# A first norm split by block, a planner that keeps GpSimd and VectorE apart, and tiles placed in the buffer that comes free first

## The chip, the core and the metric

The kernel runs on one core of one Trainium2 chip. Its time is the device time of one execution in microseconds; the times below are the median of several executions. The engines are TensorE (PE in the views; its weight loads are PEld), VectorE (DVE), ScalarE (ACT), GpSimd (POOL) and SyncE (SP, which only issues transfers here). ScalarE's queue issues some transfers as well.

## What is computed

One transformer block with the norm after each half, in float32: grouped-query attention with normed queries and keys and a distance bias, then a gated feed-forward with integer weights. Batch 2, sequence 512, width 512; 32 query heads, 8 key and value heads of 128; feed-forward width 1376.

```python
q = rmsnorm((x @ Wq.T) per head, q_norm_w);  k = rmsnorm((x @ Wk.T) per head, k_norm_w);  v = x @ Wv.T
scores = q k^T / sqrt(128) + (-1e30 above the diagonal, slope_h * (key - query) below it)
x = layernorm(x + (softmax(scores) v) @ Wo.T)
h = silu((x @ gate_w.T) * gate_s) * ((x @ up_w.T) * up_s)
out = layernorm(x + (h @ down_w.T) * down_s)
```

## The kernel before

**Units and pairs.** A unit is (group g, batch b, block i): the four query heads of one key and value head, and one block of 128 rows. Two units in a row make a pair, so there are 64 units and 32 pairs. A pair is projected together: 256 rows by 768 columns (four query heads, one K, one V).

**Seven products.** Nearly every projection is done as a two by two block product with seven multiplications in place of eight (`seven`, with `PLAN`). A product is named in the text by the first number of its row in `PLAN`; they are issued as 1, 2, 6, 7, 4, 5, 3. Products 1, 6, 7 and 4 add up in one PSUM bank (`pa`), 5 and 3 in another (`pb`), 2 has its own (`pc`); between them the bank is copied or added to SBUF, so product 6 waits for the copy of product 1. The factors need sums of blocks first: `sx` of the input, `tq` of the projection weights, `to` of the output weights, `so` of the attention output, `sw`, `tx`, `sh` and `td` in the feed-forward part. Those are two-input sums in SBUF, that VectorE or GpSimd can do (`sums_a`, `sums_b`, through `tensor`, L520).

**The first pair** is projected the plain way (`project_plain`, tiles `pp`): four banks, four chunks `kc` of the depth, for each chunk the blocks of rows r = 0, 1 and the halves of columns n = 0, 1. A float32 product of 384 columns is two matmul instructions.

**Norm of a pair** (`heads`): ScalarE squares the five heads of each block (L766), VectorE adds them up (`ms<-sq`, L775) and scales (L782), GpSimd raises to the power -1/2 (`inv<-ms`, L506), two multiplies give the normed heads (`sq<-c,inv`), and TensorE turns them (`ptq` for queries, L836; `ptk` for keys, L858). `qT` and `kT` are their copies.

**Attention of a unit**: four score products (`sc<-kT,qT`, L889), on each a bias add with row maximum on VectorE (L898), an exponential on ScalarE (L914), a rescale on GpSimd (`pr<-pr,rden`, L946), transposes (`pt`, L978), copies (`prT`), products with v (`pa<-prT,v`, L997). Then the output projection adds into `y`, and after the last group the layer norm follows.

**Feed-forward part.** For each of 11 chunks of the width and each batch: weights loaded as integers and cast (`wf`), sums `sw`, seven products (`pa_h`, `pb_h`, `pc_h`) whose banks are copied by ScalarE and added by VectorE into `gu`, a sigmoid (L1366), and two three-operand products of VectorE (`sg`, L1374; `hT`, L1383). A bank must be emptied before its next product.

**The order of work** is made by a planner, `Work`. The kernel records every operation with the engines that could do it, an estimated duration for each, and a priority. `emit` then steps through a list schedule: among all operations whose inputs are done it takes the one, and the engine, that can start earliest by the estimates, with priority as the next criterion, and issues it there. So each engine's instruction order is fixed when the program is built. The engines then run in their own order and wait for each other through semaphores; the estimates do not bind them. An operation that needs a new tile takes the next one of its ring (`Ring`), in turn; it has to wait until all users of the tile that held that place are done.

The planner's estimates for two-input sums in SBUF are `dve(n, sbuf=True)` on VectorE and `pool_tt(n)` on GpSimd; nothing in it knows of the two engines hindering each other.

**Loads at the start.** `load_qkv(0)` issues, for each chunk, the query weights of both halves as one transfer of 256 KB on SP, and on ACT's queue the input (`load_x`, 128 KB), the K and the V weights (64 KB each). A transfer takes one of eight semaphores in turn, so a ninth waits for the first to land. Meanwhile TensorE does 16 idle transposes (`idle`, tile `warm`).

Of the kernel before, what the change touches and what calls it, by code (L numbers as in the profile page):

```python
# [58 lines left out]
def dve(n, sbuf=False):  # L59
    return 0.2 + 0.0014 * n if sbuf else 0.15 + 0.00106 * n  # L60


def pool_tt(n):
    return 0.28 + 0.0021 * n


def pool_ts(n):
    return 0.3 + 0.00095 * n
# [6 lines left out]
class Ring:  # L75


    def __init__(self, name, bufs, shape, dtype=F32, gate=None):
        self.name, self.bufs, self.shape, self.dtype = name, bufs, shape, dtype
        self.gate = gate  # L80
        self.pool = None
        self.items = []
# [14 lines left out]
class Work:  # L97
# [6 lines left out]
    def add(self, costs, prio, fn, reads=(), writes=(), after=(), table=None, lag=0.0):  # L104

        op = {
            "costs": costs,
            "prio": prio,
            "fn": fn,
            "deps": set(id(o) for o in after),  # L110
            "obj": list(after),
            "takes": [],
            "end": None,
            "table": table,
            "lag": lag,
            "n": len(self.ops),
        }
        deps = {id(o): o for o in after}
        for key in reads:
            o = self.wrote.get(key)  # L120
            assert o is not None, (key[0].name, key[1])
            deps[id(o)] = o
        for key in writes:
            o = self.wrote.get(key)
            if o is not None:
                deps[id(o)] = o
            for o in self.read.get(key, ()):
                deps[id(o)] = o
        for key in reads:
            if key not in writes:  # L130
                self.read.setdefault(key, []).append(op)
        for key in writes:
            self.wrote[key] = op
            self.read[key] = []
        bufs = []
        for key in list(reads) + list(writes):
            b = key[0]
            if b not in bufs:
                bufs.append(b)
        for b in bufs:  # L140
            op["takes"].append(b)
            b.users.append(op)
        op["deps"] = list(deps.values())
        self.ops.append(op)
        return op

    def emit(self):
# [20 lines left out]
        emitted = 0  # L168
        while ready:
            best = None  # L170
            for o in ready:
                t0 = o["at"]
                for b in o["takes"]:
                    if b.tile is not None:
                        continue
                    r = b.ring
                    if r.gate is not None and r.gate["end"] is None:
                        t0 = None
                        break
                    k = len(r.items) - r.bufs  # L180
                    if k >= 0:
                        for u in r.items[k].users:
                            if u["end"] is None:
                                t0 = None
                                break
                            t0 = max(t0, u["end"] + LAG[u["eng"]])
                        if t0 is None:
                            break
                if t0 is None:
                    continue  # L190
                for e, c in o["costs"].items():
                    s = max(t0, free.get(e, 0.0))
                    key = (s, o["prio"], s + c, o["n"])
                    if best is None or key < best[0]:
                        best = (key, o, e, c, s)
            assert best is not None, "no work can start: " + ", ".join(
                b.name for o in ready for b in o["takes"]
            )
            _, o, e, c, s = best
# [9 lines left out]
            elif e == "NONE":  # L209
                o["end"] = s  # L210
            else:
                free[e] = s + c
                o["end"] = s + c
            o["lag"] += LAG[e]
            for b in o["takes"]:
                if b.tile is not None:
                    continue
                b.ring.items.append(b)
                b.tile = b.ring.pool.tile(
                    b.ring.shape, b.ring.dtype, tag=b.ring.name, name=b.name, bufs=b.ring.bufs  # L220
                )
# [11 lines left out]
def post_ln_block(  # L233
# [122 lines left out]
    def load_qkv(g, prio):  # L356
# [3 lines left out]
        for kc in range(NK):  # L360
            load(
                0.26,
                prio + 0.01 * kc,
                lambda q, kc=kc: q.dma_start(w[:, kc, :, : 2 * HD], src[:, kc]),
                [(w, ("q", kc))],
            )
            if g == 0:
                load_x(0, kc, 0, prio + 0.01 * kc, "ACTQ")
                for n, other in enumerate((wkt, wvt)):
                    load(  # L370
                        0.066,
                        prio + 0.01 * kc + 0.001,
                        lambda q, kc=kc, n=n, other=other: q.dma_start(
                            w[:, kc, n, 2 * HD :], other[ts(kc, P), ts(g, HD)]
                        ),
                        [(w, ("kv", n, kc))],
                        queue="ACTQ",
                    )
# [12 lines left out]
    def load_x(b, kc, q, prio, queue="SP"):  # L391

        c0 = q * NTH
        load(
            0.13,
            prio,
            lambda e: e.dma_start(
                xT[b][:, kc, c0 : c0 + NTH], xt[ts(kc, P), b * S + c0 : b * S + c0 + NTH]
            ),
            [(xT[b], (kc, q))],  # L400
            queue=queue,
        )

    def w_keys(g, kcs, ns=(0, 1)):
        w = w_qkv[g]
        return [(w, ("q", kc)) for kc in kcs] + [(w, ("kv", n, kc)) for kc in kcs for n in ns]
# [20 lines left out]
    def idle(e):  # L427
        for k in range(16):
# [3 lines left out]
    W.add({"PE": 3.3}, -9.0, idle, [A(ident)], [A(warm)])  # L432
# [54 lines left out]

    def make_bias(g, prio):
        bg = Buf(r_bias, f"bias_{g}")
        bias[g] = bg  # L490
        for h in range(G):
# [7 lines left out]
                [(bg, h)],  # L499
            )  # L500

    def rsqrt(dst, src, n, prio, dst_key, src_key):
# [6 lines left out]
            [src_key, A(nhalf)],  # L509
            [dst_key],  # L510
# [4 lines left out]
    def tensor(n, prio, dst, a, b, alu, reads, writes, who=("DVE", "POOL"), sbuf=None, after=()):  # L515
        cost = {"DVE": dve(n, len(who) > 1 if sbuf is None else sbuf), "POOL": pool_tt(n)}
# [6 lines left out]
            after,  # L523
        )

    def sums_a(n, prio, s, a, s_key, a_keys):
# [5 lines left out]
        tensor(n, prio, g(0), f(1, 0), f(1, 1), add, k(1, 0) + k(1, 1), [s_key(0)])  # L532
        tensor(n, prio, g(2), f(0, 0), f(1, 0), sub, k(0, 0) + k(1, 0), [s_key(2)])
        tensor(n, prio, g(1), g(0), f(0, 0), sub, [s_key(0)] + k(0, 0), [s_key(1)])
        tensor(n, prio, g(3), f(0, 1), g(1), sub, k(0, 1) + [s_key(1)], [s_key(3)])
# [57 lines left out]
    def sums_x(b, q, prio):  # L593
        def blocks(r, k):
# [10 lines left out]
            lambda r, k: [(xT[b], (2 * k, q)), (xT[b], (2 * k + 1, q))],  # L605
# [17 lines left out]
    def sums_o(g, prio):  # L623
# [9 lines left out]
            lambda r, n: [A(w)],  # L633
        )
# [5 lines left out]
    def copy_op(n, prio, dst, src, reads, writes, who=("ACT", "DVE")):  # L640
# [6 lines left out]
        cost = {"ACT": act(n), "DVE": dve(n), "POOL": 0.2 + 0.00095 * n}  # L647
        W.add({e: cost[e] for e in who}, prio, fn, reads, writes)

    def project_plain(p, prio):  # L650
# [7 lines left out]
        for kc in range(NK):  # L658
            for (r, n), bank in banks.items():
# [10 lines left out]
                reads = [(xT[b], (kc, i // 2))] + w_keys(g, (kc,), (n,)) + ([A(bank)] if kc else [])  # L670
                W.add({"PE": pe(W3)}, prio + 0.01 * kc, mm, reads, [A(bank)])
# [10 lines left out]
    def project(p, prio):  # L682
# [50 lines left out]
        def a_keys(f):  # L733
            if isinstance(f, tuple):
                return [(xT[b], (2 * f[1], i // 2)), (xT[b], (2 * f[1] + 1, i // 2))]
# [14 lines left out]
    def heads(p, prio):  # L750
# [10 lines left out]
        nh = 2 * (G + 1)  # L761
        for r in range(2):
# [9 lines left out]
        W.add(  # L772
            {"DVE": 1.5},
            prio,
            lambda e: nc.vector.tensor_reduce(ms.tile, sq.tile, AX.X, ALU.add),  # L775
            [(sq, 0), (sq, 1)],
            [A(ms)],
        )
        W.add(
            {"DVE": 0.2},  # L780
            prio,
            lambda e: nc.vector.tensor_scalar(  # L782
                ms.tile, ms.tile, 1.0 / HD, RMS_EPS, ALU.mult, ALU.add
            ),
            [A(ms)],
            [A(ms)],
        )
        rsqrt(
            lambda: inv.tile.rearrange("p r h -> p (r h)"),
            lambda: ms.tile.rearrange("p r h -> p (r h)"),  # L790
            nh,
            prio,
            A(inv),
            A(ms),
        )
        for r in range(2):
# [7 lines left out]
                [(cb, (r, 0)), (cb, (r, 1)), A(inv)],  # L804
# [153 lines left out]
    def attend(u, prio):  # L958
# [68 lines left out]
        def halves(e):  # L1027
# [11 lines left out]
            {"PE": 0.7},  # L1039
# [87 lines left out]
    def layernorm(t, prio, dst, dst_keys, name):  # L1127
        stats, mv = Buf(r_stats, f"stats_{name}"), Buf(r_mv, f"mv_{name}")
        ve, rstd = Buf(r_ve, f"ve_{name}"), Buf(r_rstd, f"rstd_{name}")
        for n in range(2):  # L1130
# [21 lines left out]
        rsqrt(lambda: rstd.tile, lambda: ve.tile, 1, prio, A(rstd), A(ve))  # L1152
# [7 lines left out]
            dst_keys,  # L1160
        )
# [42 lines left out]
    for p in range(NP):  # L1204
# [7 lines left out]
        if p == 0 or g != pairs[p - 1][0]:  # L1212
            sums_q(g, u - 3.0)
            sums_o(g, u + 1.0)
        if p == 0:
            project_plain(p, u - 2.4)
        else:
            if g == 0 or (g == 1 and b == 0 and i == 0):
                sums_x(b, i // 2, u - 3.0)
            project(p, u - 2.4)  # L1220
        heads(p, u - 1.8)
        for k in range(2):
# [84 lines left out]
    def ffn_up(fc, b, weights, prio):  # L1307
# [52 lines left out]
        def finish():  # L1360
# [17 lines left out]
                [A(sg)],  # L1378
            )
# [12 lines left out]
                [(h, (fc, 0)), (h, (fc, 1))],  # L1392
            )
# [197 lines left out]
```

## Time and profile before

| | |
|---|---|
| median of 3 runs | 1078.73 us (1078.64 to 1078.96) |
| the profiled execution | 1081.15 us, of which its span is 1079.4 us |
| TensorE's mean granted clock in it | 0.995 |
| busy: PE / DVE / POOL / ACT | 1059.0 / 687.2 / 514.8 / 408.3 us |
| transfers | 38.93 MB, mean 36 GB/s |
| first useful product (`pp`) | at 5.35 us |
| first score product (`sc`) | at 33.72 us |

The busy time of an engine is the union of its instructions. A matmul's record lasts longer than the time until the next one may start: a 128x384 product reads 0.49 us, and such products follow each other every 0.32 us. In a timeline line the first figure is the start from the beginning of the span, the second the length, and a bracket at the end gives the idle time of that engine before it and what ended it. In a line of windows the columns are the stretch, its length, the busy time of PE, PEld, DVE, ACT and POOL (with the number of instructions), the granted clock of TensorE as a share of full speed, the share of the transfer engines and GB/s.

### The profile page before, as it was taken

Reading aid. Unit: us, or ns where it says so; the run is one execution under the profiler, and the core shown is the slowest. Engines: PE = TensorE matmul, PEld = TensorE weight load, DVE = VectorE, ACT = ScalarE, POOL = GpSimd, SP = SyncE. Lnnn points to the kernel's source line nnn. Section 1 sums busy time; section 2 is a strip of 40 time slices with the busy share of each in tenths; the row PEclk is TensorE's granted clock in tenths of the full one; section 3 lists DMA queues with packets and bytes.
Section 4 is the critical chain, followed back from the end, with each engine's and each line's share of the span. In section 5 each row is a group of like instructions: output and inputs, shape, how many; then the busy total and the mean of one; then the engine's idle time right before and its main releaser. Section 6 shows DMA issues by size and latency. Waiting matters only on the chain.

```text
span 1079.4 us, 13367 instructions
## 1 busy us (share of the span) xinstructions
PE 1059.0 (98%) x4612; PEld 763.0 (71%) x4612; DVE 687.2 (64%) x1611; ACT 408.3 (38%) x1024; POOL 514.8 (48%) x673
## 2 busy tenths in 40 slices
PE   8999999999999999999999999999999999999997
PEld 5667676667666767676666766766667787877886
DVE  7665576656665666565656567657676667677554
ACT  2534444443344434443344334343444423433100
POOL 9364454445544453545355526554666443245130
PEclk9999999999999999999999999999999999999999
DMA  8210011001200120012001200100101012320011
GB/s 273 89 46 14 1 40 51 9 1 39 60 0 1 40 59 1 1 40 60 1 1 40 59 1 1 40 1 1 39 1 39 20 51 67 103 57 20 1 40 39
DMA packets 44146, 38.93 MB, mean 36 GB/s; under 512 B 3664, under 2 KB 36432, under 8 KB 44080
## 3 DMA queue, kind: packets, MB, share of 16 engines
q1 hardware_dynamic: 42352, 37.05, 11.2%
q10 hardware_dynamic: 1728, 1.05, 0.4%
q8 instruction: 36, 0.59, 0.2%
q14 instruction: 30, 0.25, 0.1%
HBM read 35.99 MB, written 2.10 MB: 35 GB/s over the span
## 4 chain that ended last, share of the span: by engine, by line
PE 92%; DVE 4%; DMA 2%; POOL 1%; issue 1%; ACT 0%; SPq 0%; POOLq 0%; DVEq 0%; ACTq 0%
PE pa_q L568 14%; PE sc L889 12%; PE pa_o L568 10%; PE pa L997 10%; PE pb_q L568 7%; PE pt L978 6%; PE pa_h L568 5%; PE pb_o L568 5%; PE pc_q L568 4%; PE pa_d L568 3%; PE pb_h L568 3%; PE ptq L836 3%; PE pc_o L568 2%; PE px L1029 2%; PE pb_d L568 2%; PE pc_h L568 1%
## 5 line engine op out<-in xcount | busy, mean ns | idle before, releaser
L946 POOL TENSOR_SCALAR pr<-pr,rden 128x64 f32<-128x64 f32 (+12 forms) x288 | 155.3, 558 | 83.6 <-DVE rden L929 71.3
L914 ACT ACTIVATE pr<-pr,nmax 128x32 f32<-128x32 f32 (+15 forms) x256 | 132.4, 518 | 78.3 <-DVE nmax L898 76.6
L889 PE MATMUL sc<-kT,qT 128*128 128x160 f32 (+15 forms) x512 | 154.2, 407 | 0.3
L898 DVE CUSTOM_DVE_ANT_0 pr<-sc,bias 128x32 f32<-128x32 f32 (+15 forms) x256 | 108.9, 436 | 52.4 <-PE sc L889 51.3
L997 PE MATMUL pa<-prT,v 128*128 128x512 f32 (+1 forms) x320 | 136.3, 507 | 0.0
L889 PEld LDWEIGHTS sc<-kT,qT 128*128 128x128 f32 x512 | 87.0, 190 | 42.1 <-issue 25.6
L643 ACT COPY c<-pa_q 128x384 f32<-128x384 f32 x104 | 49.6, 477 | 123.5 <-PE pa_q L568 118.3
L568 PE MATMUL pa_q<-tq,sx 128*128 128x384 f32 x248 | 91.0, 489 | 0.1
L520 DVE TENSOR_TENSOR y<-y,pa_o 128x256 f32<-128x256 f32 x128 | 53.6, 419 | 50.5 <-PE pa_o L568 49.0
L978 PEld LDWEIGHTS pt<-ident,pr 128*128 128x128 f32 x576 | 68.8, 141 | 23.7 <-issue 10.8
L978 PE MATMUL pt<-ident,pr 128*128 128x128 f32 x576 | 79.4, 273 | 0.3 <-DVE prT L645 0.3
L506 POOL TENSOR_TENSOR inv<-ms,nhalf 128x10 f32<-128x10 f32 x32 | 63.8, 1993 | 21.4 <-DVE ms L782 20.5
L643 ACT COPY prT<-pt 128x512 f32<-128x512 f32 (+1 forms) x79 | 43.5, 556 | 78.9 <-PE pt L978 78.5
L766 ACT ACTIVATE sq<-c 128x640 f32<-128x640 f32 x64 | 47.2, 737 | 66.4 <-DVE c L520 64.1
L645 DVE COPY prT<-pt 128x512 f32<-128x512 f32 (+1 forms) x81 | 50.0, 621 | 33.2 <-PE pt L978 32.7
L997 PEld LDWEIGHTS pa<-prT,v 128*128 128x128 f32 x320 | 57.7, 190 | 15.1 <-issue 0.9
L645 POOL COPY v<-c 128x128 f32<-128x128 f32 x49 | 15.2, 309 | 111.5 <-DVE c L520 110.8
L568 PE MATMUL pa_o<-to,so 128*128 128x256 f32 x256 | 65.7, 379 | 0.0
L520 DVE TENSOR_TENSOR c<-pb_q,c 128x384 f32<-128x384 f32 x62 | 34.4, 554 | 48.8 <-PE pb_q L568 48.7
L568 PEld LDWEIGHTS pa_q<-tq,sx 128*128 128x128 f32 x248 | 45.0, 190 | 25.0 <-issue 6.3
L643 ACT COPY gu<-pa_h 128x256 f32<-128x256 f32 (+1 forms) x88 | 32.0, 369 | 77.0 <-PE pa_h L568 57.7
L643 ACT COPY aT<-pa 128x512 f32<-128x512 f32 (+1 forms) x48 | 26.4, 550 | 87.8 <-PE pa L997 87.8
(160 smaller groups left out, 2181.0 us busy)
## 6 DMA issues: line engine op xcount, KB each, us to landing
w<-in_wqt_dram SPq DMA_DIRECT2D x32, 256.0 KB, 4.1
wo<-in_wot_dram SPq DMA_DIRECT2D x8, 1024.0 KB, 5.5
wi<-in_gwt_dram SPq DMA_DIRECT2D x14, 256.0 KB, 2.8
wi<-in_uwt_dram SPq DMA_DIRECT2D x14, 256.0 KB, 3.2
wdi<-in_dwt_dram SPq DMA_DIRECT2D x10, 256.0 KB, 3.4
y<-in_x_dram SPq DMA_DIRECT2D x1, 2048.0 KB, 13.9
out_dram<-o SPq DMA_DIRECT2D x8, 256.0 KB, 2.0
w<-in_wkt_dram SPq DMA_DIRECT2D x7, 256.0 KB, 5.2
```

What stands on the lines that cost most here:

```text
L506: lambda e: nc.gpsimd.tensor_tensor(dst(), src(), nhalf[:, :n], ALU.pow),
L520: lambda e: vec[e].tensor_tensor(dst(), a(), b(), alu),
L568: nc.tensor.matmul(bank[:rows, :width], lhsT=a(fa, c), rhs=b(fb, c), start=(fresh and c == 0), stop=(c == depth - 1), skip_group_check=True,)
L643: nc.scalar.copy(dst(), src())
L645: vec[e].tensor_copy(dst(), src())
L766: lambda e, r=r: nc.scalar.activation(sq[:, r].rearrange("p h d -> p (h d)"), c(r)[:, : 5 * HD], AF.Square),
L889: lambda e, a=a, w=w, sc=sc: nc.tensor.matmul(sc[:, :w], lhsT=qT[:, a, :, :], rhs=kT[:, :w], start=True, stop=True),
L898: lambda e, a=a, w=w, sc=sc: nc.vector.tensor_tensor_reduce(out=pr[:, a, :w], in0=sc[:, :w], in1=bg[:, S - w :], scale=-1.0, scalar=MAX_IN ...
L914: lambda e, a=a, w=w: nc.scalar.activation(pr[:, a, :w], pr[:, a, :w], AF.Exp, bias=nmax[:, a : a + 1], scale=-1.0, accum_out=den[:, a : a ...
L946: lambda e, a=a, c0=c0, n=n, to=to, c1=c1: nc.gpsimd.tensor_scalar(to[:, a, c1 : c1 + n], pr[:, a, c0 : c0 + n], rden[:, a : a + 1], 1.0, ...
L978: nc.tensor.transpose(pt[:, ts(k, P)], pr[:, a, ts(j, P)], ident.tile)
L997: lambda e, j=j, prT=prT, n=n: nc.tensor.matmul(po[:, S - n :], lhsT=v[:, j, :], rhs=prT[:, :n], start=(j == 0), stop=(j == i), skip_group ...
```

## The change

It does five things.

1. **Norm of the first pair by block.** For pair 0 the sum, the scaling and the power are made for each of the two blocks of rows by itself (five heads each), and each block's multiply needs its own block's power only. The other 31 pairs are as before.
2. **First loads.** For chunk 0 the query weights go as two transfers of 128 KB (one on SP, one on ACT's queue), the input as two of 64 KB, and K and V on SP. Idle transposes go from 16 to 14. The input is tracked by blocks of 128 rows, and the query weights by halves, so a product waits for what it reads and no more. Block 0's products of a chunk come before block 1's.
3. **Work behind the norm.** The biases of groups from 1 on, the `to` sums of all groups, and the `sx` sums of batch 1 and of the first half of batch 0 name the first pair's two powers (`lead`) as forerunners; group 0's own bias stays ahead. `sums_o` is recorded after `heads`.
4. **Ports.** VectorE operations with two SBUF inputs are marked `port`. In the plan a GpSimd operation starts only after the last marked VectorE operation ended, and a marked one only after the last GpSimd operation. The estimates change: VectorE's two-input sums in SBUF are no longer dearer than others, and those of GpSimd are a little lower.
5. **Tiles.** A ring keeps its places by number; a new tile takes the place whose users end first by the plan, and each place is a tile of its own tag with one buffer.

```diff
-def dve(n, sbuf=False):
-    return 0.2 + 0.0014 * n if sbuf else 0.15 + 0.00106 * n
+def dve(n):
+    return 0.15 + 0.00106 * n
 def pool_tt(n):
-    return 0.28 + 0.0021 * n
+    return 0.27 + 0.00197 * n
 def pool_ts(n):
-    return 0.3 + 0.00095 * n
+    return 0.27 + 0.00083 * n
...
-        self.items = []
+        self.slots = [None] * bufs
+
+    def room(self):
+        best = None
+        for k, b in enumerate(self.slots):
+            t = 0.0
+            for u in b.users if b else ():
+                if u["end"] is None:
+                    break
+                t = max(t, u["end"] + LAG[u["eng"]])
+            else:
+                if best is None or t < best[0]:
+                    best = (t, k)
+        return best
+
+    def take(self, b):
+        k = self.room()[1]
+        self.slots[k] = b
+        b.tile = self.pool.tile(self.shape, self.dtype, tag=f"{self.name}{k}", name=b.name, bufs=1)
...
                 for e, c in o["costs"].items():
                     s = max(t0, free.get(e, 0.0))
-                    key = (s, o["prio"], s + c, o["n"])
-                    if best is None or key < best[0]:
-                        best = (key, o, e, c, s)
+                    if e == "POOL":
+                        s = max(s, port["DVE"])
+                    elif e == "DVE" and o["port"]:
+                        s = max(s, port["POOL"])
+                    at_engine.setdefault(e, []).append((s, o["prio"], s + c, o["n"], c))
...
+                if e == "POOL" or (e == "DVE" and o["port"]):
+                    port[e] = s + c
...
+            if g == 0 and kc == 0:
+                queries((0,))
+                load_x(0, kc, 0, at, "ACTQ", 2)
+                other(0, queue="SP")
+                queries((1,), queue="ACTQ")
+                other(1, queue="SP")
+            else:
+                queries((0, 1))
+                if g == 0:
+                    load_x(0, kc, 0, at, "ACTQ")
+                    other(0)
+                    other(1)
...
     def idle(e):
-        for k in range(16):
+        for k in range(14):
...
-                reads = [(xT[b], (kc, i // 2))] + w_keys(g, (kc,), (n,)) + ([A(bank)] if kc else [])
-                W.add({"PE": pe(W3)}, prio + 0.01 * kc, mm, reads, [A(bank)])
+                reads = x_keys(b, (kc,), (i + r,)) + w_keys(g, (kc,), (n,)) + ([A(bank)] if kc else [])
+                W.add({"PE": pe(W3)}, prio + 0.01 * kc + 0.004 * r, mm, reads, [A(bank)])
...
+        for rs in ((0,), (1,)) if p == 0 else ((0, 1),):
+            lo, hi = rs[0], rs[-1] + 1
+            n = len(rs) * (G + 1)
+            cut = lambda t, lo=lo, hi=hi: t[:, lo:hi]
+            keys = lambda t, rs=rs: [(t, r) for r in rs]
+            W.add(
+                {"DVE": 0.15 + 0.135 * n},
+                prio,
+                lambda e, cut=cut: nc.vector.tensor_reduce(cut(ms), cut(sq), AX.X, ALU.add),
+                keys(sq),
+                keys(ms),
+            )
...
+            if p == 0:
+                lead.append(W.ops[-1])
...
-                [(cb, (r, 0)), (cb, (r, 1)), A(inv)],
+                [(cb, (r, 0)), (cb, (r, 1)), (inv, r)],
                 [(sq, r)],
...
         if p == 0 or g != pairs[p - 1][0]:
             sums_q(g, u - 3.0)
-            sums_o(g, u + 1.0)
...
             if g == 0 or (g == 1 and b == 0 and i == 0):
-                sums_x(b, i // 2, u - 3.0)
+                sums_x(b, i // 2, u - 3.0, lead if p > 1 else ())
             project(p, u - 2.4)
         heads(p, u - 1.8)
+        if p == 0 or g != pairs[p - 1][0]:
+            sums_o(g, u + 1.0, lead)
```

The sums, the layer norm's last step (L1156) and the two three-operand products of the feed-forward part (L1374, L1383) are marked `port=True`.

## The prediction

> **What bounds the kernel now.** I read the page's shares first, then who waited for whom on TensorE, then the timeline of the places that those waits point to, and last the granted clock there.
>
> ```profile
> span 1079.4 us, 13367 instructions
> PE 1059.0 (98%) x4612; PEld 763.0 (71%) x4612; DVE 687.2 (64%) x1611; ACT 408.3 (38%) x1024; POOL 514.8 (48%) x673
> ```
>
> TensorE is the bound: it is idle for 20 us in all. The change adds and removes no matrix product (only two warm-up transposes), so it can win or lose only in TensorE's pauses and in what follows them. The waits of TensorE name these:
>
> ```profile
> PE pb_h L568 <- DVE gu L520: 3.8, 3, 2.8
> PE ptq L836 <- DVE sq L520: 2.5, 1, 2.5
> PE pa_h L568 <- ACT gu L643: 1.4, 2, 1.0
> ...
> PE pc_q L568 <- DVE c L645: 1.2, 1, 1.2
> ...
> PE pp L662 <- DMA w<-in_wkt_dram: 0.6, 1, 0.6
> PE pa_q L568 <- ACT c L643: 0.6, 1, 0.6
> ```
>
> The columns are total, times and longest. With the timeline they fall into two places. The first 34 us hold 1.34 + 0.63 + 1.19 + 0.57 + 2.52; then TensorE runs without a break until 657 us; the feed-forward part, from 893 to 993 us, holds six pauses of together 5.86. The last product's end leaves 6.6 us of layer norm and store, which nothing here touches. The start, in order of time (start, length, engine, line):
>
> ```profile
> 5.35 10.56 PE L662 MATMUL pp<-w,xT 128*128 128x384 f32 x32 [0.63 <-DMA w<-in_wkt_dram]
> ...
> 17.79 0.55 DVE L645 COPY c<-pp 128x384 f32<-128x384 f32 x1
> ...
> 18.39 1.56 PE L568 MATMUL pc_q<-w,xT 128*128 128x384 f32 x4 [1.19 <-DVE c L645]
> ...
> 19.51 1.47 DVE L775 TENSOR_REDUCE ms<-sq 128x10 f32<-128x1280 f32 x1
> ...
> 24.33 2.16 POOL L506 TENSOR_TENSOR inv<-ms,nhalf 128x10 f32<-128x10 f32 x1
> ...
> 26.52 2.62 DVE L520 TENSOR_TENSOR sq<-c,inv 128x640 f32<-128x640 f32 x2 [0.93 <-POOL inv L506]
> ...
> 28.46 1.12 PE L836 MATMUL ptq<-ident,sq 128*128 128x128 f32 x4 [2.52 <-DVE sq L520]
> ```
>
> The norm of the first pair is one chain: a late copy, a reduce over both blocks, a power on GpSimd that stands behind a `to` sum, two multiplies. TensorE stops for it at 25.94, and pays again afterwards:
>
> ```profile
> 28.46:31.77 3.31, 3.31 (x9) 2.15 (x9) 1.15 (x2) 1.31 (x2) 0.29 (x1) 0.53 0.89 280
> ```
>
> The third figure from the end is the clock, 0.53: 3.31 x 0.47 = 1.6 us are lost while TensorE counts as busy. The largest later pause has its cause on VectorE:
>
> ```profile
> 968.80 1.99 POOL L520 TENSOR_TENSOR sh<-hT,sh 128x640 f32<-128x640 f32 x1
> ...
> 969.32 1.75 DVE L520 TENSOR_TENSOR sw<-wf 128x256 f32<-128x256 f32 x1
> ...
> 970.99 1.21 DVE L1383 SCALAR_TENSOR_TENSOR hT<-gu,us_sb,sg 128x512 f32<-128x512 f32 x1
> ...
> 972.46 0.41 DVE L520 TENSOR_TENSOR gu<-pb_h,gu 96x256 f32<-96x256 f32 x1
> ...
> 973.01 1.36 PE L568 MATMUL pb_h<-x1T,sw 128*96 128x256 f32 x4 [2.83 <-DVE gu L520]
> ```
>
> A 128x256 sum that takes 0.41 alone takes 1.75, ending just after GpSimd's; the 0.41 us eviction for which TensorE waits stands behind it. The clock falls here too (0.53 from 973.49 to 976.90, another 1.6 us).
>
> **What the Trainium skill says.** "SBUF — State Buffer", section "SBUF: two separate sides": VectorE with two SBUF inputs and GpSimd share ports under an exclusive lock, held for the whole instruction. The 1.75 against 0.41 agrees. "TensorE: Matmul & The Clock Gate", section "What's actually happening": the clock halves after an idle window of about 3.4 us. The halving agrees, the length does not quite: here 2.52 and 2.83 us of idle did it, 1.19 us did not. "GPSIMD Engine Reference", section "4.1 Engine selection": two-input work is about twice as slow on GpSimd; here a 128x640 multiply takes 1.51 against 0.81. "DMA: Bandwidth & Descriptors", section "Latency and other measured facts": about 2 us of fixed cost; the smallest load here (`kw`, 0.5 KB) takes 2.4 from issue to landing, so no product can start before 0.72 + 2.4 = 3.1.
>
> **Part 1, first loads.** Chunk 0 goes from four issues to six (SP: half of `wqt`, `wkt`, `wvt`; ACT's queue: half of x, the other half of `wqt`, half of x), at 0.47 us an issue. The first product now needs 128 + 64 + 64 KB, first and second on their queues. In the trace the first 384 KB landed by 4.26 and the last piece that the first product needed at 5.22. With the same rate the 256 KB, with the 128 KB issued beside them, are there at about 4.3; the 14 warm-up transposes (two fewer; 13 of 16 ran at half speed, until 4.17) end at about 4.5. I take 4.6 for the first product, bounds 4.3 and 5.3. What is moved back: on SP chunk 1's weights from 1.2 to 2.2, on ACT's queue chunk 1's K and V behind the eight-semaphore limit. Needs come every 2.58 us (8 instructions x 0.3225): K and V of chunk 1 at 7.2 and 7.8 (landed at 6.56 and 7.40), of chunk 2 at 9.8 and 10.4 (8.6, 8.95), of chunk 3 at 12.3 and 13.0 (11.0, 12.0). Half a microsecond later still fits; 1 us later costs at most the 0.7 gained.
>
> **Part 2, norm by block, and the order around it.** In the instruction order of the changed kernel, the `pp` group takes 10.32 from 4.6 to 14.9, block 0 first. ScalarE's two copies and square (0.48, 0.48, 0.74) end at 15.3. VectorE, which GpSimd no longer hinders since it has nothing to do before 14.4, does three `tq` sums of 0.96 and one `sx` of 0.72 from 12.0 (the last V) to 15.7 instead of 17.8, then the copy of block 1 (16.3), half a reduce (0.75, half of 1.47: 17.05), the scaling (0.17) and the copy of product 1 (17.85). Product 6 waits for that copy: TensorE arrives at 17.5, so about 0.45 of idle in place of 1.19. GpSimd: two `sx` sums and a copy until 17.6, a power on five (from ten at 1.99 and one at 0.6: estimate 1.2) to 18.8, the multiply of block 0 at 1.51 to 20.3; the second power to 21.5; VectorE's multiply of block 1 0.82 to 22.4. TensorE has products 6, 5 and 7 (3 x 1.29) until 21.8, so `ptq` of block 0 is 1.4 early, and `ptk` (wanted at 23.5) 1.1 early. The wait and the half clock both go. Late next: product 6 only. The first score product stands, after products of 1.29 each and the transposes, at 26.8, against 33.7 now, with the same 21.7 us of TensorE work before it: the losses fall from 12.0 to 5.05, which is 6.9. Because every step of VectorE is queued, I take **6.5**; bounds 4.5 (VectorE 2 us later) and 7.3.
>
> **Part 3, what was moved behind the norm.** The bias of group 1 (4 x 0.64 = 2.6 us of GpSimd), the `to` sums (four, 0.69 to 1.53) and the `sx` sums of batch 1 and batch 0's first half (twelve, 0.41 to 0.77) now come after it. Behind them in GpSimd's queue stand the second pair's power and the first rescale of `pr`: I count them done at 33.8 and about 35.5, and TensorE wants the transposes of `pr` at 26.8 + 8.55 = 35.4. At nothing, or 0.8 lost; cover is the four products of projection 2 and one of 3.
>
> **Part 4, the scheduler over the rest.** Every engine's order changes, and tiles are put in other buffers. From 34 to 657 us nothing can be won, for TensorE has no pause there; a loss is possible. In the feed-forward part GpSimd gets fewer two-input sums (its 128x256 `sw` sums go from 35 to 25, and it does nine 128x512 casts instead of 13), and around the 973 us pause two such sums instead of six stand beside the evictions. What can come back: pauses 0.27 + 0.91 + 5.86, 0.17 each for the refill of eight pauses (a product ends 0.17 after the next could start: 0.38 against 0.215), and the 1.6 of clock: 10 us. The trace of before cannot show which go. From above it is 8 (two or three short ones stay), from below minus 2 (new ones as long as the present ones' average, with no clock loss). I take 4, and 0.8 for losses of parts 3 and 4 before 657 us.
>
> **Sum.** 6.5 + 4.0 - 0.8 = 9.7. The profiled execution took 1081.15 (1.75 around its span), so 1071.4 on its own account; it lies 2.4 above the median of the runs, 1078.73. From the median: **1069.0**.
>
> **Rivals.** (a) Only the start is won; new waits in the feed-forward part equal the old: 1078.73 - 6.5 + 0.8 = 1073. For it: the planner's durations are estimates, and an engine that runs half a microsecond off plan makes the lock again. Against: its new two-input figures (0.42 for 256, 0.69 for 512) are those of undisturbed rows. (b) Slower: the planner, now holding GpSimd back whenever VectorE has a two-SBUF-input operation, plans the rescale of `pr` (L946) just in time, and TensorE waits for it at L978. There are 32 pairs; one wait of 0.33 with its refill in each gives back 10.6. At 0.7 a pair it is 22 us against 10.5 won: about 1090. It decides from 0.3 us a pair on. Against: GpSimd is idle half of the time, ScalarE 62%, and TensorE's queue holds projection products between the two. (c) The start doesn't do what it says: the K load lands at 5.3 as now and VectorE's `tq` sums come 2 us later than I count, so that product 6 and the norm wait again; with nothing won later, 1077 to 1079.
>
> **How the numbers follow.** Both parts won 0.58 (1069), (a) 0.29 (1073), (c) 0.06, (b) 0.07. The range 1064 to 1075 takes in the bounds of the first two: 7.3 + 8 won is 1063.5, 4.5 with 0.8 lost is 1075. Within 0.2% (2.2 us, about what a measurement of this kernel can tell from no change) lies most of (c): faster 0.88, same 0.05, slower 0.07.
>
> **What would show it.** Right: first `pp` at 4.3 to 5.3; power and reduce of the first pair in two of five; no wait of `ptq` above 0.3; clock near 1.0 from 28 to 32; first `sc` at 26 to 29; no wait of `pb_h` above 1. Wrong: a wait of TensorE for `pr` repeated in every pair, or a clock below 0.9 in a slice after the first.

## The result, and the profile after

The changed kernel takes **1061.67 us** (median of 6 runs, 1061.52 to 1062.39) against 1078.85 for the kernel before in the same comparison (6 runs, 1076.98 to 1080.89): a ratio of 0.9839, interval 0.9827 to 0.9852. The gain is 17.2 us; the forecast was 9.7, in a range of 1064 to 1075. The direction was right, the size was not.

The changed kernel's profiled execution took 1061.77, close to its median. The one of before took 1081.15, which is 2.3 above its median. So the two traces differ by 19.4, of which 2.2 belongs to that one execution of before. Of the runs of the kernel before whose mean granted clock is on record, all that took more than 1080 us have 0.995 or 0.996, and all others at least 0.997. All differences of traces below are on the account of the two traces.

The page's shares of the kernel after:

```profile
span 1060.0 us, 13371 instructions
PE 1050.8 (99%) x4610; PEld 762.2 (72%) x4610; DVE 654.2 (62%) x1603; ACT 421.6 (40%) x1054; POOL 455.2 (43%) x654
```

VectorE is 33 us less busy and GpSimd 60 us less, with nearly the same work; ScalarE is 13 us busier, with 30 instructions more. TensorE's waits, complete this time (total, times, longest):

```profile
PE warm L482 <- POOL ident masks.py:199: 1.3, 1, 1.3
PE pa_d L625 <- DVE y L576: 0.5, 1, 0.5
PE pa L1063 <- ACT prT L702: 0.5, 1, 0.5
PE pa_h L625 <- ACT gu L702: 0.5, 1, 0.5
PE pa_q L625 <- DVE c L704: 0.4, 1, 0.4
```

No wait of `ptq` or `pb_h` is left, and only one of `pa_h`. The start of the kernel after, from its timeline (start, length, engine, line):

```profile
4.38 11.27 PE L721 MATMUL pp<-w,xT 128*128 128x384 f32 x32
...
15.57 0.55 DVE L704 COPY c<-pp 128x384 f32<-128x384 f32 x1
...
16.04 0.80 DVE L839 TENSOR_REDUCE ms<-sq 128x5 f32<-128x640 f32 x1
...
17.64 1.20 POOL L562 TENSOR_TENSOR inv<-ms,nhalf 128x5 f32<-128x5 f32 x1
...
18.16 1.53 PE L625 MATMUL pa_q<-tq,sx 128*128 128x384 f32 x4
...
18.92 1.26 POOL L576 TENSOR_TENSOR sq<-c,inv 128x640 f32<-128x640 f32 x1
...
22.11 0.60 PE L902 MATMUL ptq<-ident,sq 128*128 128x128 f32 x4
...
27.08 0.55 PE L955 MATMUL sc<-kT,qT 128*128 128x32 f32 x4
```

The reduce and the power are over five heads, no line of TensorE shows a wait in brackets, and the first score product comes at 27.08 instead of 33.72. The clock did not fall; two lines of the windows, whose figure before the last two is the clock:

```profile
24.00:28.00 4.00, 4.00 (x21) 2.81 (x19) 3.34 (x9) 2.51 (x5) 1.64 (x2) 1.00 1.07 382
28.00:32.00 4.00, 4.00 (x18) 2.66 (x17) 3.00 (x12) 2.26 (x10) 3.73 (x8) 1.00 1.01 320
```

A stretch of the feed-forward part of the kernel after, at about the place in a chunk where before had its pause of 2.83:

```profile
954.01 0.41 DVE L576 TENSOR_TENSOR sw<-wf 128x256 f32<-128x256 f32 x1
...
954.46 0.42 DVE L576 TENSOR_TENSOR gu<-pb_h,gu 96x256 f32<-96x256 f32 x1
...
955.47 0.41 DVE L576 TENSOR_TENSOR sw<-sw,wf 128x256 f32<-128x256 f32 x1
955.58 1.03 PE L625 MATMUL pb_h<-x1T,sw 128*96 128x256 f32 x4
955.62 0.84 POOL L576 TENSOR_TENSOR td<-wd,td 128x256 f32<-128x256 f32 x1 [2.08 <-DVE td L576]
...
956.43 0.72 POOL L576 TENSOR_TENSOR sw<-wf,sw 128x256 f32<-128x256 f32 x1
```

VectorE's sums take 0.41 and `pb_h` starts without a bracket. GpSimd's second sum stands beside evictions of PSUM and takes 0.72. Its first still overlaps a VectorE sum, from 955.62 to 955.88, and takes 0.84: the plan keeps such pairs apart, but the engines run a little off its times.

**A table of losses.** The idle time of TensorE doesn't account for 19.4 us, so I measured all the time that it lost. For each product shape I took the median time from one product's start to the next in the kernel after, and summed these "undisturbed" times in program order. The loss at a point is the time on the clock less that sum. It counts pauses, refills and slow clock alike. Cut at 40, 640 and 820 us of work done (the last part is mostly the feed-forward part, and ends in about 6 us of layer norm and store that all kernels have):

| kernel | median, us | ratio to before [interval] | to 40 | 40-640 | 640-820 | 820-end | all |
|---|---|---|---|---|---|---|---|
| before | 1078.85 | | 10.4 | 6.9 | 4.3 | 16.3 | 37.9 |
| after | 1061.67 | 0.9839 [0.9827, 0.9852] | 4.4 | 4.1 | 2.6 | 7.6 | 18.7 |
| start_only | 1076.56 | 0.9976 [0.9969, 0.9984] | 5.0 | 8.3 | 4.2 | 16.2 | 33.7 |
| plan_only | 1065.45 | 0.9891 [0.9875, 0.9907] | 7.4 | 4.1 | 2.5 | 7.8 | 21.8 |
| no_port | 1078.16 | 0.9988 [0.9977, 0.9999] | 9.5 | 6.5 | 6.6 | 12.8 | 35.4 |
| turns | 1074.07 | 0.9960 [0.9947, 0.9973] | 5.0 | 11.2 | 4.9 | 9.8 | 30.9 |
| neither_new | 1086.45 | 1.0075 [1.0060, 1.0090] | 8.2 | 14.4 | 7.9 | 12.3 | 42.8 |
| old_cost | 1066.16 | 0.9887 [0.9873, 0.9902] | 4.2 | 7.4 | 4.3 | 7.2 | 23.1 |
| f_turns | 1073.93 | 0.9961 [0.9947, 0.9975] | 4.6 | 11.2 | 4.6 | 9.7 | 30.1 |
| f_free | 1060.91 | 0.9838 [0.9823, 0.9853] | 4.3 | 4.1 | 2.6 | 6.9 | 17.9 |
| whole_norm | 1062.10 | 0.9849 [0.9832, 0.9867] | 4.3 | 4.1 | 2.6 | 7.6 | 18.6 |
| old_loads | 1061.42 | 0.9846 [0.9827, 0.9864] | 4.7 | 4.1 | 2.5 | 7.8 | 19.1 |
| no_lead | 1061.12 | 0.9840 [0.9819, 0.9861] | 3.9 | 4.0 | 2.6 | 7.7 | 18.2 |
| norm_and_lead | 1063.62 | 0.9853 [0.9833, 0.9873] | 5.7 | 4.0 | 2.6 | 7.6 | 19.9 |
| norm_and_loads | 1061.73 | 0.9836 [0.9813, 0.9859] | 3.7 | 3.9 | 2.5 | 7.8 | 17.9 |
| best | 1060.09 | 0.9820 [0.9801, 0.9839] | 3.4 | 4.1 | 2.6 | 6.9 | 17.0 |

The first two rows say where the time came from: 6.0 from the start, 4.5 from the middle (2.8 and 1.7), 8.7 from the end; 19.2 in all.

### The profile page after: what moved, and what is told of

The parts are those of the page before. It is cut to its first block, busy times and chain, and to the rows that moved or that the text cites. A ratio compares the mean times of both kernels' runs of the same rounds, so it can differ in the third digit from the quotient of the medians.

```text
span 1060.0 us, 13371 instructions
## 1 busy us (share of the span) xinstructions
PE 1050.8 (99%) x4610; PEld 762.2 (72%) x4610; DVE 654.2 (62%) x1603; ACT 421.6 (40%) x1054; POOL 455.2 (43%) x654
## 4 chain that ended last, share of the span: by engine, by line
PE 99%; DVE 0%; issue 0%; ACT 0%; POOLq 0%; POOL 0%
PE pa_q L625 15%; PE sc L955 12%; PE pa L1063 10%; PE pa_o L625 10%; PE pb_q L625 8%; PE pa_h L625 7%; PE pt L1044 6%; PE pb_o L625 5%; PE pc_q L625 4%; PE pb_h L625 4%; PE pa_d L625 3%; PE ptq L902 3%; PE pc_o L625 3%; PE px L1095 2%; PE pc_h L625 2%; PE pb_d L625 2%
## 5 line engine op out<-in xcount | busy, mean ns | idle before, releaser
L1012 POOL TENSOR_SCALAR pr<-pr,rden 128x64 f32<-128x64 f32 (+12 forms) x288 | 138.5, 500 | 56.0 <-DVE rden L995 45.1
L702 ACT COPY prT<-pt 128x512 f32<-128x512 f32 (+1 forms) x112 | 58.6, 529 | 112.7 <-PE pt L1044 111.8
L702 ACT COPY c<-pa_q 128x384 f32<-128x384 f32 x113 | 53.7, 476 | 119.5 <-PE pa_q L625 119.1
L562 POOL TENSOR_TENSOR inv<-ms,nhalf 128x10 f32<-128x10 f32 (+1 forms) x33 | 63.3, 1917 | 3.8 <-DVE ms L846 2.7
L625 PEld LDWEIGHTS pa_o<-to,so 128*128 128x128 f32 x256 | 45.3, 191 | 9.5 <-issue 1.0
L704 DVE COPY prT<-pt 128x512 f32<-128x512 f32 (+1 forms) x48 | 32.7, 681 | 27.3 <-PE pt L1044 27.2
```

The costliest lines, as they stand in the source:

```text
L562: lambda e: nc.gpsimd.tensor_tensor(dst(), src(), nhalf[:, :n], ALU.pow),
L625: nc.tensor.matmul(bank[:rows, :width], lhsT=a(fa, c), rhs=b(fb, c), start=(fresh and c == 0), stop=(c == depth - 1), skip_group_check=True,)
L702: nc.scalar.copy(dst(), src())
L704: vec[e].tensor_copy(dst(), src())
L1012: lambda e, a=a, c0=c0, n=n, to=to, c1=c1: nc.gpsimd.tensor_scalar(to[:, a, c1 : c1 + n], pr[:, a, c0 : c0 + n], rden[:, a : a + 1], 1.0, ...
```

## The experiments

Theory: the start is worth about 6.5 and comes from the loads, the norm and its order; the rest comes from the exclusion of the ports. Rivals: the placement of tiles does it; the new estimates do it; any reshuffling does it.

**Which part of the planner?** Four kernels, each the changed one with parts put back.

start_only (planner, estimates and tiles as before):

```diff
-                    if e == "POOL":
-                        s = max(s, port["DVE"])
-                    elif e == "DVE" and o["port"]:
-                        s = max(s, port["POOL"])
...
-        best = None
-        for k, b in enumerate(self.slots):
+        k = len(self.items)
+        for u in self.items[k - self.bufs].users if k >= self.bufs else ():
...
-    return 0.15 + 0.00106 * n
+    return 0.2 + 0.0014 * n if sbuf else 0.15 + 0.00106 * n
```

> Parts 1 to 3 of the change alone (first loads, norm by block, work behind the norm); planner, estimates and tile placement as before. Theory (the start is worth 6.6 us, the exclusion of the ports the remaining 10.5): 6.6 won, 1072, and pauses in the feed-forward part as before, about 6 us. Rival 'luck' (the pauses of before were an accident of one order, which any reshuffling removes): part of the feed-forward gain comes here too, 1066 or less.

Measured 1076.56: neither case, for 2.4 were won where 6.6 was expected. Its losses to 40 us of work fall from 10.4 to 5.0, but 1.4 more come after it (40-640: 8.3 against 6.9), and its end loses what before loses (16.2 and 16.3). The two lines of the feed-forward pauses stand in its waits with nearly the same figures as before:

```profile
PE pb_h L616 <- DVE gu L567: 3.8, 3, 2.8
PE pa_h L616 <- ACT gu L693: 1.4, 2, 0.9
```

This run can't decide on the rival 'luck', however. From about 200 us on TensorE, VectorE, ScalarE and GpSimd have their order of before (of VectorE's 1615 instructions the last 1312), so the feed-forward part was not reshuffled. It was in no_port and neither_new below, both without the exclusion: they lose 12.8 and 12.3 in the last part, against 16.3 before and 7.6 after. Another order alone thus brought up to 4.0 there, and these include 1.6 of half clock that neither of the two traces has in that part; it did not bring the whole 8.7.

plan_only (parts 4 and 5; the start as before):

```diff
-            if g == 0 and kc == 0:
+            if False:
...
-        for rs in ((0,), (1,)) if p == 0 else ((0, 1),):
+        for rs in ((0, 1),):
...
-                lead.append(W.ops[-1])
+                pass
```

> Parts 4 and 5 alone (ports, estimates, placement); first loads, norm and their order as before. Theory: 10.5 won, 1068, first score product still at about 33, no pause above 1 us after 600 us. If the parts do not add up (the planner is what wins the start too, by clearing GpSimd before the first norm), it is 1064 to 1066.

Measured 1065.45, the second case: the parts do not add up, and the first score product comes at 30.99, not at about 33. From 40 us on its losses are those of the kernel after, within 0.2 in each column: everything after the start comes from parts 4 and 5. They also win 3.0 inside the start.

no_port (the four lines of the exclusion are left out, all else stays):

> The changed kernel without the exclusion: the marks are there, the planner does not look at them; new estimates and placement stay. Theory (exclusion does it): loses most of 10.5, 1070 to 1072, feed-forward pauses return, 128x256 sums on VectorE of 1.2 us and more return. Rivals 'placement' and 'estimates': at most 2 us lost, 1062 to 1064.

Measured 1078.16: without the exclusion nearly the whole gain is gone, more than expected. VectorE's sums are longer again: of those of 128x256, 44 of 116 take over 0.6 us, against 13 of 111 in the kernel after and 41 of 97 before. The timeline at its largest feed-forward pause shows what follows:

```profile
965.29 2.00 POOL L572 TENSOR_TENSOR sh<-hT,sh 128x640 f32<-128x640 f32 x1
...
965.93 2.05 DVE L572 TENSOR_TENSOR sh<-hT,sh 128x640 f32<-128x640 f32 x1
...
967.90 0.41 DVE L572 TENSOR_TENSOR gu<-pc_h,gu 96x256 f32<-96x256 f32 x1
968.24 0.41 DVE L572 TENSOR_TENSOR gu<-pb_h,gu 128x256 f32<-128x256 f32 x1
...
968.67 0.72 ACT L1430 ACTIVATE sg<-gu,gs_sb 128x512 f32<-128x512 f32 x1 [3.92 <-DVE gu L572]
...
969.30 0.35 ACT L698 COPY gu<-pa_h 96x256 f32<-96x256 f32 x1
...
969.70 1.10 PE L621 MATMUL pa_h<-tx,sw 128*96 128x256 f32 x4 [2.08 <-ACT gu L698]
```

VectorE's `sh` sum, for which the kernel after has 0.82 where it stands alone, takes 2.05 beside GpSimd's, which holds until 965.29 + 2.00 = 967.29. Two evictions stand behind it, ScalarE's sigmoid waits for them (3.92 idle), the copy of `pa_h` stands behind the sigmoid, and TensorE waits 2.08 for that copy. It is the pattern that the prediction showed at 968 us of the kernel before, with one link more. Lengthened sums stand ahead of the next two pauses too. Before the one of 1.94 at 32.44, three 128x256 sums beside GpSimd's take 3.15 together (27.80 and 30.87), where 0.41 each would be 1.2. Before the one of 1.64 at 890.34, an `sw` sum that takes 1.48 (888.47) stands in front of the eviction that TensorE waits for.

turns (tiles in turn; exclusion and estimates stay; the second hunk of start_only):

> The changed kernel with tiles taken in turn, as before. Theory (exclusion): unchanged within 1.5 us, 1061 to 1063. Rival 'placement' (an operation that is ready waits for a place in turn while another place is free): loses 5 us or more, 1067 and above.

Measured 1074.07: the rival that I had given no weight holds as well. The exclusion alone is far from enough. The added loss is largest in the middle (11.2 against 4.1). A pause comes back in nearly every group (the waits list seven, 4.1 in all; five of them, 3.1, in the middle):

```profile
185.63 1.45 PE L620 MATMUL pa_q<-tq,sx 128*128 128x384 f32 x4
...
187.18 0.48 ACT L697 COPY c<-pa_q 128x384 f32<-128x384 f32 x1 [0.71 <-PE pa_q L620]
...
187.71 0.94 PEld L620 LDWEIGHTS pa_q<-tq,sx 128*128 128x128 f32 x4 [1.24 <-ACT c L697]
187.71 1.56 PE L620 MATMUL pa_q<-tq,sx 128*128 128x384 f32 x4 [0.62 <-ACT c L697]
```

These are products 6 and 7. They follow each other with nothing between them, so 7 waits for the copy of 6. In the kernel after, TensorE has other work at the same place:

```profile
181.15 1.45 PE L625 MATMUL pa_q<-w,xT 128*128 128x384 f32 x4
...
183.90 1.45 PE L625 MATMUL pc_q<-w,xT 128*128 128x384 f32 x4
185.19 1.45 PE L625 MATMUL pa_q<-tq,sx 128*128 128x384 f32 x4
...
186.91 1.03 PE L625 MATMUL pb_o<-to,so 128*128 128x256 f32 x4
...
189.30 1.45 PE L625 MATMUL pa_q<-tq,sx 128*128 128x384 f32 x4
```

Product 2 (`pc_q`) stands between 1 and 6, and products of the output projection between 6 and 7. In turns product 2 comes later than 7. That it waited there for the bank whose turn it was, while another was empty, is how the rule works in the plan; the traces show the order only.

**Do the two add up, and which tiles matter?** neither_new leaves out both the exclusion and the first-free placement:

> The changed kernel without the exclusion and with all tiles in turn; the new estimates stay. With exclusion alone 1074.1, with first-free alone 1078.2, with both 1061.7. If the two add up, this is 1090; if each is of use only together with the other, it is 1074 to 1080.

Measured 1086.45, slower than before, and nearer to the sum than to the other case. With the new estimates the four medians are:

| | tiles in turn | first free |
|---|---|---|
| no exclusion | 1086.45 | 1078.16 |
| exclusion | 1074.07 | 1061.67 |

Exclusion wins 12.4 or 16.5, placement 8.3 or 12.4; each is worth 4.1 more with the other. In neither_new the wait that rival (b) of the prediction named does appear, though nine times and not in every pair:

```profile
PE pt L1035 <- POOL pr L1003: 2.3, 9, 0.5
```

old_cost (exclusion and placement stay, the estimates of before return; the third hunk of start_only and the like):

> The changed kernel with the estimates of before (a two-input sum of 640 columns 1.10 instead of 0.83 on VectorE, 1.62 instead of 1.53 on GpSimd, the others alike). Theory (exclusion and placement make the plan come true, whatever its figures are within a tenth or three): 1062 to 1064. Rival 'estimates' (a plan that keeps engines apart by wrong lengths inserts idle time and puts operations in a wrong order): 1067 or more.

Measured 1066.16: 4.5 lost, neither as little nor as much as the two cases said. All of it is lost ahead of 820 us of work (7.4 and 4.3 against 4.1 and 2.6). Beside start_only and neither_new this shows what the old figures did. Without exclusion and placement they are better than the new ones, 1076.56 against 1086.45; with both they are worse, 1066.16 against 1061.67. One reading, which is argued and not shown: a dearer two-input sum on VectorE stands in for the lock as long as the plan does not know of the lock, and leaves room unused as soon as it does.

f_turns and f_free split the placement: the ring `f`, three PSUM banks that hold all products of seven before the feed-forward part, half of those in it, and three of the first pair's four; and all other rings.

```diff
     def room(self):
+        if self.name == "f":
+            k = len(self.items)
+            ...
+            return (t, k % self.bufs)
```

> The changed kernel with one ring alone taken in turn: f, the three PSUM banks of the products. Theory 'banks' (all that first-free placement wins is that a product need not wait for the bank whose turn it is while another is empty): as the kernel with all rings in turn, 1073 to 1075, with a wait of product 6 for a copy once in every group. Rival 'SBUF tiles' (tq, to, so, sq, prT and the like decide): 1061 to 1065.

> The reverse: every ring in turn except f, whose banks go to whichever comes free first. Theory 'banks': 1061 to 1063, as the changed kernel. Rival 'SBUF tiles': 1070 or more.

Measured 1073.93 and 1060.91. Theory "banks" holds on both sides: the three banks alone account for the 12.4 (12.3 here), with the same pause as in turns (0.62 at 187.32), and the other rings for nothing (f_free is even 0.8 quicker, for one pause of `pa_h` fewer). Its edit is the condition turned round, `self.name != "f"`.

**Which part of the start?** whole_norm, old_loads and no_lead each undo one of parts 1 to 3 (the hunks of plan_only, one at a time; old_loads with 16 idle transposes, no_lead with `sums_o` recorded where it was):

> The changed kernel with the first pair's norm undivided (one reduce and one power over ten heads); loads and the work behind the norm stay. With parts 4 and 5 alone TensorE waited 2.8 us for the heads' multiplies, and parts 1 to 3 together won 3.1 there. If dividing the norm is what wins it: 1063.7 to 1065, first score product at about 29 and a wait of ptq or ptk above 1 us. If keeping other work behind the norm is enough: 1061.5 to 1062.5.

> The changed kernel with the first loads of before and 16 idle transposes. If the first product's start carries through: 0.7 to 1.1 lost, 1062.4 to 1062.8, first product at 5.3 to 5.5. If VectorE's chain sets the end of the start anyway: unchanged, 1061.5 to 1062.

> The changed kernel with nothing held behind the norm, and the to sums recorded where they were before. If sums would again stand ahead of the first power on GpSimd: 1 us or more lost, ptq waits. If the new planner puts them elsewhere anyway: 1061 to 1062.

Measured 1062.10, 1061.42, 1061.12: none of the three is needed, while all three together were worth 3.8 (1065.45). norm_and_lead and norm_and_loads undo two at a time:

> The changed kernel with the first pair's norm undivided and nothing held behind it; the first loads stay. Each of the two alone undone cost nothing (1062.1, 1061.1). If they stand in for each other (one of them is enough to bring the heads in time): about 3 us lost, 1064 to 1065, a wait of ptq or ptk above 1 us. If the loads are what the new planner lacks: 1061 to 1062.

> The changed kernel with the norm undivided and the first loads of before; work is still held behind the norm. If norm and lead stand in for each other: 1061 to 1062.3. If an early first product and the divided norm stand in for each other: 1064 to 1065.

Measured 1063.62 and 1061.73. Dividing the norm and holding work behind it stand in for each other, though the loss with both undone is 2.0 and not 3. The loads matter little as long as one of the two stands. With both undone they are worth 1.8, which is what lies between norm_and_lead and plan_only (1065.45). The third combination, loads and held work undone together, was not run. With norm and held work undone, GpSimd's `to` sums run beside the heads' multiplies (norm_and_lead, timeline):

```profile
22.72 1.38 POOL L576 TENSOR_TENSOR to<-wo,to 128x512 f32<-128x512 f32 x1 [0.87 <-DVE to L576]
22.89 3.70 DVE L576 TENSOR_TENSOR sq<-c,inv 128x640 f32<-128x640 f32 x2
...
24.07 1.84 POOL L576 TENSOR_TENSOR to<-wo 128x512 f32<-128x512 f32 x1
...
25.87 1.86 POOL L576 TENSOR_TENSOR to<-wo,to 128x512 f32<-128x512 f32 x1
...
26.64 0.14 PEld L924 LDWEIGHTS ptk<-ident,sq 128*128 128x128 f32 x1 [1.66 <-DVE sq L576]
26.64 0.33 PE L924 MATMUL ptk<-ident,sq 128*128 128x128 f32 x1 [1.47 <-DVE sq L576]
```

Two multiplies of 0.82 take 3.70: GpSimd's sums end at 24.10 and 25.91, the second multiply at 26.59, 0.68 after the latter, and `ptk` waits. The lock costs time here too. By its rule the plan never puts these two side by side; but it only fixes each engine's order, so here the engines must have run off its times.

best joins the two edits that gained by themselves, f_free and no_lead:

> Only the banks f first-free, every other ring in turn, and nothing held behind the norm: the two edits that were quicker than the changed kernel alone (1060.9 and 1061.1). If they add up, 1060.2 to 1060.6; if not, 1060.8 to 1061.7.

Measured **1060.09** (1060.07 to 1060.47), a little better than the lower case. Its runs lie wholly under those of the changed kernel (1061.52 and up), but in another comparison; the two ratios, 0.9820 and 0.9839, have intervals that overlap.

## Why the prediction was right or wrong

**Part 1, first loads.** First `pp` at 4.38, forecast 4.6: right, near the lower bound. But the start didn't carry through. The first products run at half pace, 0.64 instead of 0.32 us apart, until 6.13, while those of before run at full pace from 5.75: at 8 us of work both kernels have lost 3.6 to 3.7. When full pace comes differs from trace to trace, whatever the loads: with the new ones it is there at 4.29 in f_free and at 7.34 in start_only, with the old ones at 5.39 in norm_and_loads and at 7.35 in old_loads. So one trace can't price the loads, and the medians give them nothing (old_loads 1061.42, norm_and_loads 1061.73), except where norm and held work are both undone.

**Part 2, norm by block.** Forecast 6.5 and `sc` at 26.8; measured 33.72 - 27.08 = 6.6. The waits of `ptq` and the half clock went as said. Product 6 waited 0.1 (18.16 instead of 16.77 + 1.29) where 0.45 was forecast, and GpSimd's multiply took 1.26 where 1.51 was used: that figure is a mean over 18 multiplies of before, of which nine took 1.25 or 1.26 and the others up to 1.89. So the size was right, in part by luck, since the half pace took back what these terms gave; and its causes were not those of the text: the planner alone wins 3.0 of it (plan_only), parts 1 to 3 alone win 5.4 (start_only), and the divided norm, to which the part is given, is worth nothing while work is held behind it (whole_norm). I credited one edit with what either of two brings.

**Part 3, work behind the norm.** Forecast 0 to 0.8 lost. The wait of `pa_q` for `c` at 36.64 (0.43) is new, and with nothing held behind the norm it is gone and the losses to 40 us are 0.5 less. The size was right, the place was not: the transposes of `pr`, for which the loss was forecast, come at 35.83 without a wait. Whether the held work makes the new wait is open, for in old_loads, where work is held too, it is absent.

**Part 4, the rest.** This is the step that failed, in two terms. *The pool of late pauses.* I counted 10 us after 657 us and took 4, because the trace of before could not tell which pauses go. From 640 us of work on, the loss fell by 1.7 + 8.7 = 10.4: as much as the whole pool, beyond the upper bound of 8. Of it 6.1 is idle time (7.6 before, 1.5 after), 1.6 the half clock, and the other 2.7 refills and short delays. *The middle.* "From 34 to 657 us nothing can be won, for TensorE has no pause there" took idle time for the loss. Between 40 and 640 us of work before loses 6.9 and after 4.1: 2.8 won where I had put 0.8 lost. Most of these are delays of 0.06 to 0.25 us at a product: 106 of them before, 13.5 us in all, and 84 after, 10.8 us. Idle time shows hardly any of it (0.5 before), because a matmul's record outlasts the time until the next may start. The two terms make 6.4 + 3.6 = 10.0 on the account of the traces, where the sum of 9.7 stands against 19.4; the start gave 6.0 for the 6.5 of the forecast.

Against the median the forecast was short by 7.3 only (1069.0 and 1061.67). I laid the sum of one execution, 2.4 above the median, on the median, while the changed kernel's execution stands at its own median; about 2.3 of what the trace of before could lose was not in its typical run. One stretch at half clock more than usual (1.6) would make most of this, and the clock of the runs fits it; it is not shown, since only this run of before was traced.

**The reason behind Part 4** was right in kind. The lock, which the Trainium skill describes in "SBUF — State Buffer", section "SBUF: two separate sides", stands behind the pauses traced in no_port, and without the exclusion 16.5 us come back. Wrong was to treat the estimates as the doubt and the placement as a risk: put back alone, the banks cost 12.3, and I priced a tile placed first-free at nothing.

**Rivals.** (a) fell: one wait of 0.5 in place of 5.86. (b) fell for this kernel: no `pt` waits for `pr`. (c) fell: nothing of the start was lost to late sums.

## What to carry to other kernels

When a list schedule decides the order, ask two questions of it: does the plan stall by its own rules (a bank taken in turn while another is empty), and do the engines do what the plan says (a lock that it doesn't know)? Here the first was cured by placement, the second by putting the lock in the plan, and one without the other gave up most of the gain. For a kernel whose bound engine reads 98% busy, measure the loss from the spacing of that engine's instructions, not from its idle time; and if two edits protect one wait, don't give its worth to one of them.

## What the hardware showed that I had not expected

Here a VectorE operation with one SBUF input waits for GpSimd too. The scaling of `ms` (128 partitions of 5 or 10 elements, a multiply and an add by constants) takes 0.17 alone. In the kernel after, where it isn't marked as `port`, it reads:

```profile
388.02 1.81 POOL L576 TENSOR_TENSOR tq<-w,tq 128x768 f32<-128x768 f32 x1
...
388.59 1.26 DVE L846 TENSOR_SCALAR ms<-ms 128x10 f32<-128x10 f32 x1
```

It ends 0.03 after GpSimd's sum (388.02 + 1.81 and 388.59 + 1.26), and eight of its 33 take over 1.2. The Trainium skill, "SBUF — State Buffer", section "Who interferes with whom", says that `tensor_scalar` can enter modes in which it contends for the shared ports; this trace agrees that it waits, and doesn't show in which mode it ran. It cost little: at 16.88 it takes 0.68 where the prediction has 0.17, and the copy that product 6 waits for (0.1) stands behind it; TensorE's other waits do not stand behind a lengthened scaling.

The power on GpSimd takes 1.20 on 128x5 and 1.96 on 128x10 (1.99 before). And the granted clock in the records reads 1.00 from 4.38 to 6.13, while products follow each other at half pace; at the start that record doesn't show the pace.
